# A C3-style block with attention and a pruned depthwise layer: the first pointwise convolution by seven quarter products, one reciprocal for two heads, and another order of pieces

## The chip, the cores and the metric

The kernel runs on one NeuronCore of one Trainium2 chip. The metric is the device time of one execution in microseconds. The kernel before was timed three times: 2596.55, 2593.97 and 2596.15 us, with a median of 2596.15 us. All data is fp32. The profile counts two MATMUL records, and two weight loads, for each fp32 matrix product that the program issues.

## The reference

For each of eight images x (512 channels, 32 by 32 pixels):

```python
x = x + conv_block(group_norm(x))
x = x + pruned_depthwise_block(group_norm(x))
```

The first block is what the change touches:

```python
t = silu(bn(conv1x1(x, cv1_w)))            # 512 -> 512 channels
ys = [t[:, :256], t[:, 256:]]
for i in range(2):
    z = silu(bn(conv3x3(ys[-1], m_cv1_w[i])))          # 256 -> 256
    q, k, v = conv1x1(z, m_qkv_w[i])                   # 4 heads of 64
    a = softmax(q.T @ (k + r) * 64 ** -0.5)            # 1024 x 1024 for each head
    z = silu(bn(conv1x1(a @ v, m_cv2_w[i])))
    ys.append(ys[-1] + z)
return silu(bn(conv1x1(concat(ys), cv2_w)))            # 1024 -> 512
```

The second block is a depthwise 3x3 convolution, a relu, a pruning by each channel's maximum, a 1x1 convolution from 512 to 512 channels, a relu and a second pruning.

## The kernel before

**Layout.** Channels lie on the 128 partitions in chunks, and the 1024 pixels of an image along the free dimension. The images are done one after another. The 3x3 convolutions use a transformed form (`conv3`, pieces `d`, `P`, `R`, `B`, `E`). The last 1x1 convolution of the first block for images 1 to 6 (`quartered`), and the 1x1 convolution of the second block for images 0 to 6 (`layer1_back` through `by_quarters` and `one_pair`), are done as seven products of quarters in place of eight, with sums of the quarters before and after. The weights' sums are made once in the first image, stored in DRAM (`combine_weights`, `combine_more`) and read back as tiles of a ring.

**The first 1x1 convolution, `cv1` (line 684).** All eight images do it as plain matrix products: for each of four output chunks m and each half n of the pixels, four products over the input chunks k. Chunks 2 and 3 (tiles `ps_cv1`) go to `yp[0]`, the input of the first 3x3 convolution; chunks 0 and 1 (tiles `ps_y0`) go to `y0`, which is not read until the last 1x1 convolution. The profile leaves out the numbers at the end of names, so `ps_cv1` and `ps_cv2` both stand as `ps_cv`, and `ps_y0` as `ps_y`.

**Attention (line 971).** One layer has 32 steps (two pairs of heads m, two halves of the queries ih, eight blocks of keys jt). Each step makes scores (`s`, four 64x64 matrix tiles side by side), exponentials on ScalarE (`e`), a running sum on VectorE (`p`) and the products with the values (`w`). For each pair of heads `n` then sums over the partitions with a matrix of ones (tile `ps_dn`), `nr` takes reciprocals in four pieces of 128 columns, `ns` spreads them over the partitions with two transfers through SyncE's queue (tile `rw`), `sc` scales z, and `nc` lets ScalarE check the range. The 1x1 convolution `m` of `cv2m` follows.

**Order.** Nothing schedules the work at run time. Every helper only appends pieces (small functions) to lists by a short name, and `go` (line 310) calls them in the order of a text: `FIRST` for image 0, `HEAD` and `TAIL` for images 1 to 6, `HEAD` and `LAST` for image 7. `HEAD` begins with the first 1x1 convolution of the image; the second block of the image before is spread through it (taps `t`, products `o` and `O`). `TAIL` holds the last 1x1 convolution (`Q`) and the normalisation of the next image (`g`, `ga`). The class `Engines` keeps TensorE, VectorE, ScalarE and SyncE in this order, so each is one queue; the waits between them follow from the tiles.

**Buffers.** PSUM has two double banks (`big`), three single banks (`acc`: the quarter products, the values, `m`) and one (`mm`: `ps_dn` and the small sums of the normalisations). SBUF has 11 work tiles and a ring of 5 weight tiles; `ring_load` issues the next transfer of `ring_sources` (line 388) when a tile has been used up.

Of the kernel before, what the change touches and what calls it, by code (L numbers as in the profile page):

```python
# [11 lines left out]
AF = mybir.ActivationFunctionType  # L12
# [3 lines left out]
P = 128  # L16
# [29 lines left out]
    g*6 gm gd gv g gp g gb gm gd ga gv ga c gp fo gb c ta0 ga ta0 ga ta0 ti0 fo ta2 to0*2 c  # L46
    ti0*2 ca ta2*2 c rl ca ta1*3 ti2 ti1 to1 d ti1 d y ya to1 ti1 y ya ti2 to2 d y ti2 d to2 rl
    ya y d*2 ya d P Rc R P d*3 Rc R d*2 P Rc R B P Rc R B*2 P*2 Rc R E Ez B Rc R E Ez k*2 X k dw
    ta0 ka k kp ka ta0*2 v kp ti0 v va ti0 v ti0 q v va ta1 q ta1 qa q*2 qa ta1 s e s e p to0 s
    e p w to0 s e w*2 ti1 s e p ti1*2 p s e p w s to1 s e p w e p w s w to1 ta2 e s e w h p z  # L50
    ta2 s e p ta2 s ti2 e w*2 s e w ti2 to2 ti2 s e w s e to2 w s e w s e w s e rh p w p*5 h z
    s*2 w e*2 n s e w p s p w nr e p w nr*2 s e nc s nr e ns p w s e p w*2 nc s e p w h z s e s
    w s*2 p*2 e w p e*2 p sc p w sc s w e p w s e p w*3 h z n nr*4 ns nc sc Q K m ma sc dp mr
    m*2 ma mr m ma mr ma mr d*4 Q nc K d*3 P d P Rc R d*2 Rc R d*2 P Rc R P*2 Rc B R B P Rc R E
    Ez Rc B*2 R E Ez k X dx k*3 ka*2 kp*2 v*2 q v*2 va*2 cw*3 rk cw q*2 qa q qa s*2 e*2 p s e p
    w s e w s p cw*2 e s e w s e p rk p w s e p*2 s e w s e g*2 w*2 p w h z s e w cw s e p*2
    cw*2 rk s e w*2 s e w s*2 p e rk w p s e g w p g p s*2 e g w g e*2 p w h z p s w e g p w n
    nr s e nr p w g s e s p w nr e s e w p w*2 s nr p e s e w h ns p s e p nc*2 s w e p w s e p
    w s e p w s sc e p s e p w sc w*3 h z n nr*2 Q nr*2 ns z Q sc*2 nc m*2 ma mr ma mr m ma nc m
    ma mr gm mr gd Q gv u A Q x u i A x i gp i*2 Q gb ga*4 Q im id Q iv A Q x ip i*2 ib b bm t*3  # L60
    Q A t x i*2
# [3 lines left out]
    t c*2 t b im id bm c ca iv t ip t l t*2 ib lr b t*3 c bm ca b y d y bm d ya d*2 ya d*3 y P d  # L65
# [60 lines left out]
def fast_kernel(  # L126
# [111 lines left out]

    r_dram = [dram.tile([P, 2, HW], F32, tag=f"r{l}", name="r") for l in range(2)]

    ones = const_tile([P, 32], "ones")
    nc.gpsimd.memset(ones, 1.0)

    rng = const_tile([P, B * 2 * HEADS], "rng")
# [1630 lines left out]
```

## Time and profile before

| | |
|---|---|
| median of three runs | 2596.15 us |
| the profiled execution, from its first to its last instruction (its span) | 2593.6 us |
| TensorE busy | 2557.7 us |
| VectorE busy | 2054.9 us |
| ScalarE busy | 1214.4 us |
| mean granted TensorE clock | 0.997 |
| DMA | 268.51 MB, 104 GB/s on average |

What the runtime adds around the profiled execution's span is not in the profile; the median of the runs is 2.55 us longer than this span. A duration in a row of the profile runs from an instruction's start to its end. TensorE and VectorE start the next instruction before the last has ended, so the distance between starts, and not the duration, is what an instruction costs in a full queue.

### The profile page before, as it was taken

To read this page: it belongs to the slowest core of one execution; us is meant where nothing else is said; L and a number is where in the kernel's file an instruction comes from. 1 tells how busy PE (TensorE), PEld (TensorE's weight loads), DVE (VectorE), ACT (ScalarE), POOL (GpSimd) and SP (SyncE) were. 2 spreads that over 40 slices of the span, in tenths; PEclk is the share of its full clock that TensorE was granted. 3 is DMA by queue.
4 is the path that set the end of the run, shared out by engine and by line. 5 is a ranking of instruction groups with operands and counts; after the bars stand their busy time and mean duration, and the time that the engine had idled before them with its cause. 6 is when DMAs were issued, how large, how long until landed. Compare 5 with 4: busy or idle time off the path is not lost.

```text
span 2593.6 us, 36377 instructions
## 1 busy us (share of the span) xinstructions
PE 2557.7 (99%) x14806; PEld 1292.0 (50%) x14806; DVE 2054.9 (79%) x2954; ACT 1214.4 (47%) x1551; POOL 129.2 (5%) x99
## 2 busy tenths in 40 slices
PE   8999999999999999999999999999999999999997
PEld 5454463634636346463464635545355544645443
DVE  8887588877897877877778778787788877888657
ACT  3635446353463544635445444544445454363534
POOL 1000000000100000000000000000001000010000
PEclk9999999999999999999999999999999999999998
DMA  9445230522305214060140702306122151312300
GB/s 347 157 155 203 66 122 25 167 98 73 113 27 199 66 65 122 17 247 18 65 122 17 248 18 81 105 24 241 33 96 75 61 204 34 130 45 82 122 17 34
DMA packets 83791, 268.51 MB, mean 104 GB/s; under 512 B 7072, under 2 KB 37536, under 8 KB 69408
## 3 DMA queue, kind: packets, MB, share of 16 engines
q1 hardware_dynamic: 76032, 248.01, 27.2%
q0 software_dynamic: 4032, 14.68, 3.1%
q10 hardware_dynamic: 3552, 3.41, 0.4%
q8 instruction: 118, 1.93, 0.3%
q14 instruction: 57, 0.47, 0.1%
HBM read 212.34 MB, written 36.96 MB: 96 GB/s over the span
## 4 chain that ended last, share of the span: by engine, by line
PE 95%; DVE 3%; ACT 1%; issue 0%; DMA 0%; SPq 0%; DVEq 0%; ACTq 0%
PE ps_av L105 16%; PE ps_s L105 16%; PE ps_c L105 13%; PE ps_cv L105 12%; PE ps_qk L105 8%; PE ps_cv2q L105 8%; PE ps_q L105 7%; PE ps_v L105 4%; PE ps_y L105 4%; PE ps_m L105 4%; PE ps_dn L105 1%; ACT qy L105 1%; DVE sum L105 1%; DVE ht L105 1%; PE ps_pw L105 0%
## 5 line engine op out<-in xcount | busy, mean ns | idle before, releaser
L105 ACT ACTIVATE e<-ps_s 128x1024 f32<-128x1024 f32 x512 | 509.7, 1023 | 286.8 <-PE ps_s L105 265.6
L105 PE MATMUL ps_s<-qy,kr 64*64 64x512 f32 x4096 | 513.7, 592 | 1.4
L105 DVE TENSOR_TENSOR sum<-sum,e 128x1024 f32<-128x1024 f32 x384 | 475.2, 1238 | 39.2 <-ACT e L105 19.9
L105 PE MATMUL ps_av<-e,vt 64*64 64x512 f32 x4096 | 506.2, 590 | 0.0
L105 DVE SCALAR_TENSOR_TENSOR ht<-xn,v_sb,ht 128x961 f32<-128x961 f32 (+1 forms) x256 | 317.3, 1247 | 8.6 <-ACT ht L105 5.0
L105 PEld LDWEIGHTS ps_s<-qy,kr 64*64 64x64 f32 x4096 | 160.5, 132 | 289.0 <-issue 191.1
L105 PEld LDWEIGHTS ps_av<-e,vt 64*64 64x64 f32 x4096 | 165.4, 133 | 277.4 <-issue 266.0
L105 PE MATMUL ps_qk<-z,wring 128*128 128x512 f32 x512 | 231.1, 596 | 2.0 <-ACT z L105 1.3
L105 DVE TENSOR_TENSOR sum<-e 128x1024 f32<-128x1024 f32 x64 | 78.1, 1220 | 164.0 <-ACT e L105 162.6
L105 ACT COPY c<-ps_c 128x256 f32<-128x256 f32 x96 | 35.6, 371 | 259.4 <-PE ps_c L105 259.3
L105 PEld LDWEIGHTS ps_qk<-z,wring 128*128 128x128 f32 x512 | 95.6, 190 | 115.7 <-issue 101.5
L105 DVE RECIPROCAL r<-ps_dn 128x128 f32<-128x128 f32 x128 | 113.7, 925 | 11.2 <-PE ps_dn L105 9.0
L105 PE MATMUL ps_c<-vt,wring 128*128 128x128 f32 x1024 | 119.4, 276 | 2.3 <-DVE v L105 1.3
L105 PEld LDWEIGHTS ps_c<-kr,wring 128*128 128x128 f32 x1024 | 116.8, 192 | 8.0 <-issue 6.1
L105 PEld LDWEIGHTS ps_c<-vt,wring 128*128 128x128 f32 x1024 | 116.2, 192 | 4.3 <-ACT c L105 2.3
L105 PE MATMUL ps_c<-qy,wring 128*128 128x128 f32 x1024 | 117.0, 275 | 0.0
L105 PE MATMUL ps_c<-kr,wring 128*128 128x128 f32 x1024 | 117.0, 275 | 0.0
L105 PE MATMUL ps_cv<-pt,w_sb 128*128 128x512 f32 x256 | 116.7, 607 | 0.0
L105 PE MATMUL ps_v<-wring,z 128*128 128x256 f32 x512 | 115.9, 379 | 0.7 <-DVE kr L105 0.7
L105 PEld LDWEIGHTS ps_c<-qy,wring 128*128 128x128 f32 x1024 | 115.6, 192 | 0.0
L105 PE MATMUL ps_m<-z,wm_sb 128*128 128x512 f32 x256 | 112.5, 592 | 0.0
L105 PE MATMUL ps_y<-pt,w_sb 128*128 128x512 f32 x256 | 112.3, 592 | 0.0
(178 smaller groups left out, 3255.5 us busy)
## 6 DMA issues: line engine op xcount, KB each, us to landing
wring<-u SPq DMA_DIRECT2D x96, 1024.0 KB, 4.8
pt<-in_x SPq DMA_DIRECT2D x32, 512.0 KB, 9.4
rw<-r SPq DMA_DIRECT2D x64, 256.0 KB, 3.4
xt<-in_x SPq DMA_DIRECT2D x32, 512.0 KB, 7.5
out<-xt SPq DMA_DIRECT2D x32, 512.0 KB, 8.0
kr<-r POOLq DMA_DIRECT2D x28, 512.0 KB, 6.6
wring<-q SPq DMA_DIRECT2D x14, 896.0 KB, 4.6
wring<-in_wqkv SPq DMA_DIRECT2D x16, 768.0 KB, 4.4
```

The source lines that it names most:

```text
L105: made = method(*args, **kwargs)
```

## The change

Five things are changed.

1. For images 1 to 7 the first 1x1 convolution is done as two times seven quarter products through `by_quarters` and `one_pair` (the new `quartered_cv1`; pieces `ct` for the sums of the input's quarters, `c ck cu ca` for the first pair of output chunks, `y yk yu ya` for the second). Image 0 keeps `cv1`. The sums of the weights are made in image 0 by a second `combine_more` and come through the ring: two more tiles of 896 KB for each later image. The sums of the inputs are written to the tile that held the plain weights (`w1_sb`), and to `z`.
2. The sums of the softmax (`sums`) put the four quarters of each head's 512 columns into four neighbouring partitions, with 16 products of 128 columns in place of 4 of 512; so one reciprocal of 128 columns (`reciprocal`) takes the place of four. `spread` needs eight transfers of 64 KB in place of two of 256 KB, and `check` reads 128 columns in place of 512.
3. A new piece `S` has ScalarE evaluate a Silu of one number ahead of the `ma` pieces, as `X` already does with Exp.
4. `ones` becomes 36 columns, of which every fourth is one.
5. The four texts of pieces stand in another order. `HEAD` and `TAIL` are shown here, `FIRST` and `LAST` change likewise.

```diff
...
 HEAD = """
-    t c*2 t b im id bm c ca iv t ip t l t*2 ib lr b t*3 c bm ca b y d y bm d ya d*2 ya d*3 y P d
-    Rc R d*2 P Rc R d ya P d Rc R B P Rc R P B*2 Rc R E P Ez Rc B R E Ez y k*3 ya k ka X lp ka
-    kd*2 t*5 v*2 l t va v*2 va t lr q*2 t*2 lp t q qa s q e qa s e p s t e w t s e w l s*2 p*2 w
-    e*2 p w s p e s w t s w t e s e p lr e p w*2 h z s e p w s t w s p s e p e*2 w*2 p s e w s t
-    e p s w p s e w e t p*2 w lp t h z s*2 e*2 w s*2 n e p*2 e w*2 s nr s p e w nr e p s e w nr
-    s nr t p ns l w e p*2 w lr lp w ot h s e s w p ot w s w s e*2 p*2 e w p s e w s e ot p*2 z
-    sc w nc w*2 h n nc o O nr ok Ok z nr*2 sc nr ns o ou oa O*2 Ou sc Oa m sc nc m*2 ma*2 m ma
-    mr ot mr ma mr o nc mr ou d Ou o O d ou Ou o d O ou*2 oa Ou*2 d Oa o O P d*2 Rc d*3 R P d*2
-    Rc R d P Rc P R B Rc P B Rc P R B*2 Rc R ou E oa Ou R Oa o O dp E Ez*2 X k v k v ou oa Ou
-    fr*2 Oa ka kd f*2 fr*2 f*2 dx va k v*2 k va q*4 ka kd qa*2 s*3 e*2 p e w p s e w s*2 e*2 p*3
-    w s*2 g e*2 w*2 s p e w*2 s e w p s*2 h g e g p w s w z p e*2 s w e g*2 s*2 w*2 p e*2 g p*3
-    g s w*2 e p s e w h s*2 e*2 p z p w*2 s p e p s n nr*3 w e s g e p w p s w*3 e p s nc e nr s
-    ns e nc w s h s p w z w e p s e w s p e*2 p sc s w e p*2 w s sc e p w*3 h n nr*4 ns z
+    c*4 ck cu ct*2 ca cu t im c cu*2 c*2 id iv cu y ca t cu*2 ca yk ca y*2 ip y t*2 d yu d ya y
+    ib yu d*2 P d yu d*2 b P Rc R b bm d P d*2 y Rc R Rc b d R d B P Rc l B lr R B P Rc R E B P
+    Rc R E Ez*2 yu bm*2 y lp yu ya yu*2 k t*19 v*2 va k*2 ya*2 ka k ka v*2 va X l kd q*2 qa lr lp
+    t kd q s e t q qa s e p w s e s e p w*2 s*2 e*2 w s*2 w*2 s e*2 w s w e*2 s p*5 h e l w s*2 w
+    e*2 lr t s w*2 p*2 e s e s e t w s w*2 z e s*2 e w e s w s*2 h e p e w s*2 p*5 z w e*3 s*2 e
+    t w e p*2 s*2 e*2 w*2 l lr w p ot s p*2 e p*3 lp w h z n nr nc ns p*2 w lp w s*2 w e s w*2
+    e*2 w*3 p sc p sc nc S p ot h z n nr o ok o ns O Ok ou oa ot*2 O sc m sc ma m ma Ou Oa m mr
+    ma m ma O o mr*3 Ou ou d o d ou o O*2 d*2 P Ou ou Ou d*2 o ou d Rc ou nc R oa d*2 Ou oa P Rc
+    d nc O P R d*2 P Rc P R B Oa Rc P R Ou Oa B*2 Rc B Rc R E R E Ez*2 o O k*4 ou oa Ou Oa ka*2
+    fr*3 v*2 va q*2 v*2 dp qa g va g q X kd f g f kd s e q qa fr f*2 dx s e w s*2 e w e s*2 w s*2
+    e*4 p*2 w s g*3 p*3 g s w*2 e s w*2 e*2 s*2 w g h s w e*2 w p*4 s*2 w s*2 w p*2 s*2 e p w e*6
+    p w*2 h s*2 e*2 z p*4 w p*2 s e s z e w p*2 s n nr ns e w*4 nc s nc s e w p e w h s*2 w sc w
+    e w s*2 e*3 w s p e p sc p*4 w*4 z n h z nr S ns
 """
 
 TAIL = """
-    Q*2 K r2 nc r0 Q r2 sc Q m r0 sc K m*2 ma nc mr ma m r0*2 ma mr r1*2 mr Q*3 ma mr r2 r1*2 u0
-    r2 a0 u1 gm a1 gd Q x1 u0 r3 gv x0 gp r3*2 u0 Q r3 gb u0*2 Q u0 a0 i a0 ga Q i x0*2 ga Q i
-    u0 a0 i im id ga Q iv ip u1 x0 Q u1*2 ib u1 b a1 x1 bm Q ga u1 t a1 i t Q x1 u1 i*2 a1 t i t
-    x1
+    r2 r0 Q*3 r0 sc*2 r0*2 m*2 r1 m ma gm m nc gd ma gv r1 ma r3 mr*2 K mr r2 r3 gp r2 ma mr r1
+    gb ga r1 K ga ct r2 Q r3 Q*4 u1 u0 r3 Q u0*4 Q u0 Q a1 Q a0 x0 a0 ga x0 i a0 x0 i*3 im u0 a0
+    id x1 ga ct Q iv ip Q u1 x0 ib b i u1 i bm t u1 t Q*2 u1 t*2 u1*2 a1 x1 a1*2 x1*2 i*2 nc
 """
 
...
@@ -238,8 +236,9 @@
 
     r_dram = [dram.tile([P, 2, HW], F32, tag=f"r{l}", name="r") for l in range(2)]
 
-    ones = const_tile([P, 32], "ones")
-    nc.gpsimd.memset(ones, 1.0)
+    ones = const_tile([P, 36], "ones")
+    nc.gpsimd.memset(ones, 0.0)
+    nc.gpsimd.memset(ones.rearrange("p (a b) -> p a b", b=4)[:, :, 3], 1.0)
 
     rng = const_tile([P, B * 2 * HEADS], "rng")
     rng_used = [0]
@@ -388,9 +387,9 @@
     def ring_sources():
         for b in range(B):
             for l in range(2):
-                if b and l:
+                if b:
                     for p in range(2):
-                        yield q_dram[1][p].rearrange("p q k o -> p (q k o)"), 1792
+                        yield q_dram[l][p].rearrange("p q k o -> p (q k o)"), 1792
                 for i in range(6):
                     yield u_dram[l][i].rearrange("p a b c d -> p (a b c d)"), 2048
                 yield wqkv[:, l].rearrange("p k o -> p (k o)"), 1536
@@ -721,6 +720,19 @@
         add("ca", *[lambda m=m: first_end(m) for m in (2, 3)])
         add("y", *[lambda m=m, n=n: half(m, n) for m in range(2) for n in range(2)])
         add("ya", *[lambda m=m, n=n: half_end(m, n) for m in range(2) for n in range(2)])
+
+    def quartered_cv1():
+
+        sums = [t.rearrange("p a b -> p (a b)") for t in (w1_sb, z)]
+        sums = [t[:, i * HW : (i + 1) * HW] for t in sums for i in range(2)]
+
+        def end(ps, p, low, n):
+            m = 2 * p + low
+            dst = inner(yp[0], low) if p else phases(y0[:, m, :])
+            act(dst[:, :, n * 16 : n * 16 + 16], by_phase(ps), AF.Silu, BN0 + m)
+
+        ends = [lambda ps, low, n, p=p: end(ps, p, low, n) for p in (1, 0)]
+        by_quarters((p_all, sums), ("ct", "c ck cu ca", "y yk yu ya"), ends)
 
     def conv3(l):
 
@@ -877,6 +889,7 @@
         add("Ez", *[lambda m=m: close(m) for m in range(2)])
 
         add("X", lambda: nc.scalar.activation(warm[:, 1:], warm[:, :1], AF.Exp))
+        add("S", lambda: nc.scalar.activation(warm[:, 1:], warm[:, :1], AF.Silu))
 
     def positions(l, m):
 
@@ -1030,31 +1043,37 @@
         def sums(m):
 
             dn = dns[m] = ps_mm.tile([P, 512], F32, tag="mm", name="ps_dn")
-            for i in range(4):
-                t = sm[m, i // 2]
-                nc.tensor.matmul(
-                    dn[32 * i : 32 * (i + 1), :], ones, t[:, i % 2, :], start=True, stop=True
-                )
-
-        def reciprocal(m, q):
-            if q == 0:
-                rr[m] = work_tile("r")
-            c = slice(q * 128, (q + 1) * 128)
-            nc.vector.reciprocal(rr[m][:, c], dns[m][:, c])
+            for j in range(4):
+                for i in range(4):
+                    nc.tensor.matmul(
+                        dn[32 * i : 32 * (i + 1), :P],
+                        ones[:, 3 - j : 35 - j],
+                        sm[m, i // 2][:, i % 2, j * P : (j + 1) * P],
+                        start=(j == 0),
+                        stop=(j == 3),
+                    )
+
+        def reciprocal(m):
+            rr[m] = work_tile("r")
+            nc.vector.reciprocal(rr[m][:, :P], dns[m][:, :P])
 
         def spread(m):
 
             wide = rs[m] = work_tile("rw")
             for ih in range(2):
-                twice = rr[m][half(ih), :512].unsqueeze(1).to_broadcast([HD, 2, 512])
-                nc.sync.dma_start(wide[:, ih * 512 : (ih + 1) * 512], twice)
+                for j in range(4):
+                    some = rr[m][ih * HD + j : (ih + 1) * HD : 4, :P]
+                    at = (4 * ih + j) * P
+                    nc.sync.dma_start(
+                        wide[:, at : at + P], some.unsqueeze(1).to_broadcast([HD // 4, 8, P])
+                    )
 
         def check(m, src):
 
             n = rng_used[0]
             rng_used[0] += 1
-            src = dns[m] if src == 0 else rr[m][:, :512]
-            nc.scalar.activation(rr[m][:, 512:], src, AF.Copy, accum_out=rng[:, n : n + 1])
+            src = dns[m][:, :P] if src == 0 else rr[m][:, :P]
+            nc.scalar.activation(rr[m][:, P : 2 * P], src, AF.Copy, accum_out=rng[:, n : n + 1])
 
         def scale(m, ih):
             c = slice(ih * 512, (ih + 1) * 512)
@@ -1069,7 +1088,7 @@
         add("h", *[lambda m=m, ih=ih: part(m, ih) for m, ih in both])
         add("z", *[lambda m=m, ih=ih: join(m, ih) for m, ih in both])
         add("n", *[lambda m=m: sums(m) for m in range(2)])
-        add("nr", *[lambda m=m, q=q: reciprocal(m, q) for m in range(2) for q in range(4)])
+        add("nr", *[lambda m=m: reciprocal(m) for m in range(2)])
         add("ns", *[lambda m=m: spread(m) for m in range(2)])
         add("nc", *[lambda m=m, i=i: check(m, i) for m in range(2) for i in range(2)])
         add("sc", *[lambda m=m, ih=ih: scale(m, ih) for m, ih in both])
@@ -1364,7 +1383,7 @@
 
         def decide():
             pk = ps_mm.tile([P, 512], F32, tag="mm", name="pk")
-            nc.tensor.matmul(pk[:1, :1], oks, ones[:, :1], start=True, stop=True)
+            nc.tensor.matmul(pk[:1, :1], oks, ones[:, 3:4], start=True, stop=True)
             nc.vector.tensor_scalar(flag, pk[:1, :1], P - 0.5, None, ALU.is_lt)
 
         add("rg", least, decide)
@@ -1390,12 +1409,11 @@
 
             add("rh", *[released] * 1)
             add("rk", *[lambda l=l, m=m: positions(l, m) for l in range(2) for m in range(2)])
+            combine_more(0, w1)
             combine_more(1, wpw)
             for p in range(2):
                 combine_weights(p)
             cv1(((2, (0, 1)), (3, (0, 1)), (2, (2, 3)), (3, (2, 3))))
-        else:
-            cv1(((2, (0, 1)), (2, (2, 3)), (3, (0, 1)), (3, (2, 3))))
         for l in range(2):
             conv3(l)
             qkv(l, first)
@@ -1403,6 +1421,7 @@
             cv2m(l)
         add("dx", lambda b=b: load(xt, b))
         if not last:
+            quartered_cv1()
             add("dp", lambda b=b: load(pt, b + 1))
             group_norm("g gm gd gv gp gb ga", pt, lambda c: pt[c], range(KC))
         if first:
```

## The prediction

> **What bounds the kernel.** I read the page first: busy time, then the chain that ended last.
>
> ```profile
> span 2593.6 us, 36377 instructions
> ...
> PE 2557.7 (99%) x14806; PEld 1292.0 (50%) x14806; DVE 2054.9 (79%) x2954; ACT 1214.4 (47%) x1551; POOL 129.2 (5%) x99
> ...
> PE 95%; DVE 3%; ACT 1%; issue 0%; DMA 0%; SPq 0%; DVEq 0%; ACTq 0%
> ```
>
> TensorE is busy for 99% of the span and carries 95% of the chain. VectorE's 79% is an average, so the next view is one period, from the end of one image's attention to that of the next, and the conv stage inside it (columns: stretch, its length, busy time of each engine):
>
> ```profile
> 653.30:688.70 35.40, 35.40 (x226) 27.71 (x225) 33.99 (x69) 12.87 (x24) 0.22 (x1) 1.00 0.45 157
> 583.28:899.49 316.21, 316.00 (x1846) 160.15 (x1845) 253.64 (x366) 149.50 (x192) 15.16 (x11) 1.00 0.29 96
> ```
>
> A period is 316.21 us with 0.21 us of TensorE idle. Overall VectorE has 62 us to spare, but in the first conv stage it is busy for 33.99 of 35.40 us. The chain in order of time shows the boundary (start, length):
>
> ```profile
> 639.31 6.87 PE ps_cv L105 x16
> 646.29 3.54 PE ps_cv L105 x8
> 649.95 3.54 PE ps_cv L105 x8
> 653.49 10.30 PE ps_y L105 x24
> 663.79 21.44 PE ps_c L105 x192
> 685.23 3.44 PE ps_y L105 x8
> ```
>
> Here cv1 has 16+8+8+24+8 = 64 records; eight take 3.44 us, 0.43 us each. The 13.7 us of `ps_y` are what TensorE does while VectorE prepares and finishes the 3x3 convolution. Then the sums of the softmax, and what follows the last one (VectorE, SyncE's queue and TensorE on their timelines):
>
> ```profile
> 558.64 1.90 PE L105 MATMUL ps_s<-qy,kr 64*64 64x512 f32 x16
> 560.46 1.07 PE L105 MATMUL ps_dn<-sum,ones 128*32 128x512 f32 x8
> 561.46 1.09 PE L105 MATMUL ps_av<-e,vt 64*64 64x512 f32 x8
> ```
> ```profile
> 899.56 3.39 DVE L105 RECIPROCAL r<-ps_dn 128x128 f32<-128x128 f32 x4 [1.29 <-PE ps_dn L105]
> ...
> 906.18 0.69 DVE L105 TENSOR_TENSOR z<-z,rw 128x512 f32<-128x512 f32 x1 [0.88 <-DMA rw<-r]
> ```
> ```profile
> 903.06 1.17 SPq L105 DMA_DIRECT2D rw<-r  x2
> ```
> ```profile
> 909.83 2.74 PE L105 MATMUL ps_m<-z,wm_sb 128*128 128x512 f32 x6
> ```
>
> Eight `ps_dn` records of 0.605 us each fill only 1.00 us from start to next start (560.46 to 561.46): four column strips run side by side. From the sums' end to the first `m` there are 10.4 us of other products, and the scaled z is there 3 us before it is wanted.
>
> **What the skill says.** "TensorE: Matmul & The Clock Gate", Part 3, says that products in different column groups of the array run at once, each starting some 4 ns after the last; the rows above agree (the trace has the four starts 7 ns apart). Its section "Back-to-back issue gap" says that weight loads matter more as products get shorter; here the 128-wide `ps_c`, each with its own load of 128 columns, cost 21.44/192 = 0.112 us against 0.107 for a quarter of 0.43, so a short product loses 4%. "DMA: Bandwidth & Descriptors", "Anatomy of one DMA", says that the fixed part of a transfer is mostly the wait for its completion; `rw` lands 3.4 us after issue at 256 KB and a ring tile 4.8 us at 1024 KB, which agrees: eight small transfers land hardly sooner than two larger ones.
>
> **The parts.**
>
> *Products.* 4 output chunks x 2 halves x 4 k = 32 become 2 x 7 x 2 = 28. Four fewer, eight records of 0.43 us: -3.44 us an image. Seven images: -24.0 us, on the path.
>
> *Sums on VectorE.* Added per image: four `ct` (the like `pt<-ht` row: 1.216 us) and fourteen adds (`kept<-kept,ps_q`: 0.679), 14.4 us by durations. Removed: three of four reciprocals, 16 times an image becoming 4, 12 x 0.925 = 11.1 us. The net +3.3 us is nothing beside 62 us of slack; where they stand is what matters. Queued VectorE work starts closer than its duration: four `kr<-v` take 2.43 us, 0.60 each for rows of 0.65 to 0.68.
>
> *The boundary.* I walk the new `HEAD` from the last `Q`, with 0.60 us for 512 columns, 1.15 for 1024, 0.33 for 256 on VectorE, 0.7 and 1.2 on ScalarE, and 0.4 for `Rc`. VectorE finishes `u1`, `x1`, `i` at 4.0 us, `ct` at 6.9, while TensorE does four products to 6.9. The three `acc` banks then set the pace: product five needs the bank of `a12`, free after `cu` and `ca` at 5.5, six that of `s2` (7.6), seven that of `s1` (9.3); TensorE comes at 6.9, 8.6, 10.3. No wait. The last `ca` stands behind `yk` in ScalarE's queue and ends at 15.2; two taps and `d d yu d yu d d` put the first input of `P` at 20.1, where TensorE has y's products until 20.6. Then P and y keep it until 45.5 (the loads of `d`, `yu`, `R`, `B` stay 0 to 3 us ahead of each P's buffer), the first `k` until 47.2, and the second `Ez` ends at 47.6: 0.4 us late for `v`. I take +0.4 x 7 = +2.8 us. If VectorE's steps cost their full durations, 12% more over some 44 us, the lag is 4 to 5 us, and the gain of an image is gone; that is the dear end.
>
> *Softmax sums.* 32 records of 128 columns for 8 of 512, 32 times. In four strips each strip has eight records of 0.112: 0.9 us plus the two changes of layout (about 0.2), as now. I take +0.05 us each, +1.6. If the strips did not overlap, 32 x 0.112 = 3.6 us, +2.5 each, +80 in all.
>
> *Spreading.* Reciprocal 3.39 to 0.95 us; SyncE then issues eight transfers at 0.59 us (1.17/2) instead of two. First half of z: after 0.95 + 0.1 + 4 x 0.59 it is issued, 3.2 later landed, 0.7 later scaled: 7.4 us after the sums; second half 9.7. Before `m` stand now `Q*3`, 8.6 us, where it was four pieces (10.4 us), so it holds by 1 us; the third `m` wants the second half at 12. In the first layer `o*2 O*2` give 6.9 us: 0.3 late, 7 times, +2.1. On SyncE only ring loads are queued behind, which wait for a used tile anyhow and land several products ahead. The ring: 21 tiles an image for 19; 1.8 MB more per image in 313 us is 6 GB/s on 96. Hidden; without that cover, a load is 4.8 us.
>
> *Tables.* The loads (1.28 us each, 34) mostly stand already in ScalarE's idle time; `S` is worth 0 to -2 us in all; I take -1.
>
> *Image 0.* `combine_more` again: 1 MB in, 14 stores, eight sums of 0.41 us, beside attention. It has several TensorE waits of about 1 us and the last image one of 4.7 (`ps_pw` waiting for VectorE, whose chain of taps after the last `x` keeps its length); another order can move these by +-4. I take 0.
>
> Sum on the span: 2593.6 - 24.0 + 2.8 + 1.6 + 2.1 - 1 = 2575.1; with the 2.55 us by which the median is above this span, 2577.6, say 2577.
>
> **Rivals.**
>
> *The wait hides better* (0.12): the walk's 0.4 and 0.3 vanish and the order closes some of image 0's waits: 2577 - 5 - 4 = 2568. For: the period before has 0.2 us of idle. Against: VectorE has more in a stage where it is already at 96%.
>
> *VectorE becomes the bound at the boundary* (0.13): 2 us of wait an image above the walk, +14: 2591; for 1 us, 2584. For: 33.99 of 35.40. Against: the second conv stage (`o`, `O`) already holds fourteen quarter products with their adds, without a wait.
>
> *The strips do not overlap for short products* (0.05): +80, 2655, slower. It decides from 24/32 = 0.6 to 0.75 us more per sum, that is when a group of four takes about twice its 0.112 us. Against: `ps_s` runs four tiles at once for long stretches.
>
> *The eight transfers come late* (0.04): each landing 2 us later than `rw` now, in both layers: 14 to 28 us, 2591 to 2605. Against: half the size issued before, and SyncE is idle there.
>
> My case (0.66) is 2577, itself 2570 to 2584. The range of 8 in 10 leaves out the strips, the late transfers and the ends: 2566 to 2591. This kernel's runs can tell about 0.2%, 5 us: faster is below 2590.9. Faster 0.88, same 0.04, slower 0.08.
>
> **What would show it.** The period falls to about 313.5 us, and the first convolution of all images from 512 records to 456. `ps_dn` of 128 columns: 1.0 to 1.1 us per 32 records if right, above 2 if the strips fail. At each boundary a TensorE idle of 0 to 0.5 us ahead of `ps_v`, put down to `z`; more, or idle ahead of `ps_c` put down to VectorE, is the second rival. Idle of `ps_m` on z or `rw` above 0.5 us is the fourth. Wrong altogether: a period at or above 316 us.

## The result, and the profile after

The changed kernel takes 2581.42 us (median of four runs, 2578.06 to 2582.45) beside 2595.47 us for the kernel before, timed beside it (four runs, 2593.97 to 2596.55). The ratio is 0.9945, with a 95% interval of 0.9931 to 0.9959: 14 us faster, and inside the predicted range. Its profiled execution has a span of 2580.4 us for 2593.6. The forecast was 2577, so the result is some 4 us to the slow side, and the two traces show that this is not one small miss but several large ones of both signs.

The page of the changed kernel, the same parts as shown of before:

```profile
span 2580.4 us, 38500 instructions
...
PE 2533.9 (98%) x15518; PEld 1329.0 (52%) x15518; DVE 2073.5 (80%) x2992; ACT 1207.6 (47%) x1595; POOL 126.2 (5%) x100
...
PE 72%; DVE 19%; DMA 3%; ACT 2%; issue 2%; SPq 1%; ACTq 0%; POOL 0%; DVEq 0%
```

TensorE lost 23.8 us of busy time (2557.7 to 2533.9), but the span lost only 13.2. The chain, 95% TensorE before, now runs through VectorE for 19% and through DMA for 3%. The stretches (length, then busy time of PE, PEld, DVE, ACT and POOL, the clock, the DMA share and GB/s) say where TensorE is still full:

```profile
591.74:904.98 313.24, 312.19 (x1936) 164.60 (x1940) 256.65 (x372) 148.87 (x198) 14.90 (x11) 1.00 0.31 103
640.00:714.00 74.00, 73.94 (x333) 47.29 (x331) 72.60 (x120) 34.12 (x49) 4.46 (x4) 1.00 0.42 135
```

One period, end of attention to end of attention, is 313.24 us here (316.21 before), with 1.05 us of TensorE idle (0.21 before). At the image boundary and in the first convolution after it VectorE is busy for 72.60 of 74.00 us. In the kernel before it was busy for 59.96 of 73.00 us there:

```profile
640.00:713.00 73.00, 72.92 (x355) 46.52 (x357) 59.96 (x100) 32.71 (x44) 7.30 (x5) 1.00 0.37 113
```

Most of the chain's 19% comes from this stage of each image; the end of it, in order of time (start, length):

```profile
693.68 1.34 DVE mid L103 x4
695.04 0.70 DVE y L103
695.77 1.25 ACT z L103
697.07 3.07 PE ps_v L103 x13
```

The chain follows VectorE's sums up to the last `y`, then ScalarE's `z`, then `ps_v`. Yet TensorE waits for almost nothing there: between the starts of its products, one gap of 0.22 us ahead of the `ps_v` at 697.07. VectorE and TensorE are ready at almost the same time: the second rival of the prediction, VectorE as the bound at the boundary, is close, but TensorE does not wait for it yet.

To see where the 13.2 us come from I cut each execution at the end of the last product with the values (`ps_av`) of each attention. All columns in us:

| kernel | image 0, to the end of its first attention | from there to the end of its second | image 1 | mean of images 2 to 7 | tail | span |
|---|---|---|---|---|---|---|
| before | 146.03 | 124.60 | 311.66 | 316.24 | 113.83 | 2593.6 |
| after | 148.96 | 133.45 | 309.33 | 312.90 | 111.30 | 2580.4 |
| difference | +2.93 | +8.85 | -2.33 | -3.34 | -2.53 | -13.2 |

Six periods give 6 x 3.34 = 20.0 us. Image 0 takes back 11.8. So most of what is to be explained lies in the first 283 us, where the prediction had put a zero.

The chain of the changed kernel in the second attention of image 0:

```profile
224.44 7.51 DMA ht<-in_w
...
233.57 5.58 DMA xt<-in_x
239.18 10.08 DMA ht<-in_w
...
250.91 4.31 DMA r<-pos
...
255.33 1.03 ACT e L103
```

The chain runs through transfers, one behind the other, with next to no computing between. ScalarE's timeline has the price at the end of each entry (idle before it, and what ended it):

```profile
245.93 1.94 ACT L103 ACTIVATE e<-ps_s 128x1024 f32<-128x1024 f32 x2 [4.99 <-DMA s<-scomb]
...
255.33 1.03 ACT L103 ACTIVATE e<-ps_s 128x1024 f32<-128x1024 f32 x1 [5.66 <-DMA r<-pos]
```

An exponential needs a work tile to write to. There are 11, and the sums of weights (`scomb`) and the positions (`pos`) hold theirs until their transfers have landed. ScalarE waits 4.99 and 5.66 us, and TensorE then stands idle for 2.12 and 4.88 us ahead of the scores that wait for these exponentials.

### The profile page after: what moved, and what is told of

Same layout as the page of the kernel before. It is cut to its first block, busy times and chain, and to the rows that moved or that the text cites. A ratio compares the mean times of both kernels' runs of the same rounds, so it can differ in the third digit from the quotient of the medians.

```text
span 2580.4 us, 38500 instructions
## 1 busy us (share of the span) xinstructions
PE 2533.9 (98%) x15518; PEld 1329.0 (52%) x15518; DVE 2073.5 (80%) x2992; ACT 1207.6 (47%) x1595; POOL 126.2 (5%) x100
## 4 chain that ended last, share of the span: by engine, by line
PE 72%; DVE 19%; DMA 3%; ACT 2%; issue 2%; SPq 1%; ACTq 0%; POOL 0%; DVEq 0%
PE ps_s L103 15%; PE ps_av L103 14%; PE ps_qk L103 8%; PE ps_c L103 7%; PE ps_q L103 7%; PE ps_cv L103 6%; PE ps_cv2q L103 6%; PE ps_m L103 4%; PE ps_v L103 4%; DVE ht L103 3%; DVE mid L103 2%; DVE sum L103 2%; SPq L103 1%; DVE y L103 1%; DVE vtmp L103 1%
## 5 line engine op out<-in xcount | busy, mean ns | idle before, releaser
L103 ACT ACTIVATE e<-ps_s 128x1024 f32<-128x1024 f32 x512 | 504.9, 1024 | 238.3 <-PE ps_s L103 194.7
L103 PE MATMUL ps_av<-e,vt 64*64 64x512 f32 x4096 | 518.3, 593 | 0.0
L103 DVE TENSOR_TENSOR sum<-sum,e 128x1024 f32<-128x1024 f32 x384 | 468.5, 1220 | 58.3 <-ACT e L103 31.0
L103 PEld LDWEIGHTS ps_av<-e,vt 64*64 64x64 f32 x4096 | 185.1, 133 | 254.3 <-issue 227.5
L103 PEld LDWEIGHTS ps_s<-qy,kr 64*64 64x64 f32 x4096 | 172.2, 132 | 278.6 <-issue 131.3
L103 PE MATMUL ps_q<-pt,wring 128*128 128x512 f32 x392 | 176.8, 594 | 0.0
L103 PEld LDWEIGHTS ps_q<-pt,wring 128*128 128x128 f32 x392 | 71.7, 190 | 81.0 <-issue 69.4
L103 ACT ACTIVATE m<-ps_m,bi,sc 128x512 f32<-128x512 f32 x64 | 50.0, 781 | 134.7 <-PE ps_m L103 133.6
```

The costliest lines, as they stand in the source:

```text
L103: made = method(*args, **kwargs)
```

## The experiments

The first theory on the loss in image 0 (theory 1): the loads and stores of the weight sums follow one another in SyncE's queue and through one half of one tile, and so hold work tiles. Its rival (theory 2): the eight added sums on VectorE hold it up. The other questions were what each part is worth alone, and a start-up that was longer in some kernels than in others. The stages of every experiment, read as above (in e4 only those of the fast part, as told there). Each row is one execution. The periods of a kernel agree within 2 us, but the first part of image 0 varies more from kernel to kernel, so differences of about 1 us in image 0 are not read as effects:

| kernel | image 0, first part | image 0, second part | image 1 | mean of 2 to 7 | tail | span |
|---|---|---|---|---|---|---|
| e1 | 151.51 | 124.41 | 311.31 | 316.46 | 112.73 | 2598.7 |
| e2 | 147.69 | 129.65 | 312.84 | 315.34 | 111.18 | 2593.4 |
| e3 | 147.59 | 127.48 | 309.23 | 312.88 | 111.60 | 2573.2 |
| e4 | 149.38 | 131.20 | 309.24 | 313.02 | | |
| e5 | 146.08 | 131.94 | 309.31 | 312.77 | 111.60 | 2575.5 |
| e6 | 150.13 | 124.65 | 311.70 | 316.26 | 112.67 | 2596.7 |
| e7 | 149.58 | 123.55 | 309.46 | 312.60 | 112.62 | 2570.8 |
| e8 | 147.88 | 132.57 | 309.66 | 313.40 | 111.12 | 2581.6 |
| e9 | 146.89 | 123.57 | 309.36 | 312.70 | 113.01 | 2569.1 |
| e10 | 145.94 | 123.37 | 309.34 | 312.80 | 112.58 | 2568.0 |
| e11 | 149.13 | 124.70 | 311.69 | 316.27 | 113.21 | 2596.4 |
| e12 | 151.09 | 127.47 | 312.46 | 315.58 | 112.28 | 2596.8 |

### e1: the second part alone

The kernel before with the new `sums`, `reciprocal`, `spread` and `check`, and the `ones` that they need; the order stays, and of the four pieces `nr` for a pair of heads three do nothing.

```diff
-    ones = const_tile([P, 32], "ones")
-    nc.gpsimd.memset(ones, 1.0)
+    ones = const_tile([P, 36], "ones")
+    nc.gpsimd.memset(ones, 0.0)
+    nc.gpsimd.memset(ones.rearrange("p (a b) -> p a b", b=4)[:, :, 3], 1.0)
...
-        add("nr", *[lambda m=m, q=q: reciprocal(m, q) for m in range(2) for q in range(4)])
+        add("nr", *[(lambda m=m: reciprocal(m)) if q == 0 else (lambda: None) for m in range(2) for q in range(4)])
```

> The kernel before with the second part of the change alone: 16 short products, one reciprocal, eight transfers; the order of pieces is that of before, and the one reciprocal stands where the first of the four stood. If this part costs the path nothing (the sums still take 1.0 us of TensorE, and VectorE's saved 11 us an image lie off the path): within 3 us of before. If the four strips do not overlap: 60 to 80 us slower. If VectorE was what the path waited for: 10 us or more faster.

Measured: 2599.24 us, ratio to before 1.0015 (1.0008 to 1.0022). A period is 316.46 us for 316.24 before: taking 11 us of VectorE's work from an image gains nothing in the old order, as TensorE was not waiting for it. But the kernel is slower, and the whole of it stands in the first part of image 0: 151.51 for 146.03. The loss stands ahead of the first attention, where no softmax has run yet: the first product with the values starts at 97.5 us for 92.3. This was the first sign of a second cause in image 0; e5, e6 and e11 follow it.

### e2: the second part undone

The changed kernel with the old block from `sums` to `check` and the old `ones`; the piece `nr` calls the four old reciprocals.

```diff
-        add("nr", *[lambda m=m: reciprocal(m) for m in range(2)])
+        add("nr", *[lambda m=m: [reciprocal(m, q) for q in range(4)] for m in range(2)])
```

> The changed kernel with the second part alone undone: four reciprocals and two transfers for each pair of heads, in the new order of pieces. If the new order relies on the sooner reciprocal: in the first layer of each image only 6.9 us of products stand between the sums and the first m, and with four reciprocals z is scaled about 1.5 us too late, so 8 x 1.5 = 12 us slower than the changed kernel, 2593 us, with TensorE idle ahead of ps_m or VectorE waiting for rw there. If VectorE's saving lies off the path in this order as well: 2581, no wait there.

Measured: 2598.61 us, ratio to before 1.0013 (1.0007 to 1.002), so 17 us slower than the changed kernel. With the old `ones` of 32 columns it also has the tiles where the kernel before had them, which e5 will show to be worth 3 us; beside e5 it is 20 us slower. A period is 315.34 us for 312.90. The same part that gains nothing in the old order (e1) is worth 2.44 us an image in the new one, because the new order gives the reciprocal no time. ScalarE and then TensorE behind the first sums of an attention in image 2:

```profile
765.50 0.60 ACT L103 ACTIVATE r<-ps_dn 128x512 f32<-128x512 f32 x1 [4.12 <-DVE r L103]
766.08 1.93 ACT L103 ACTIVATE e<-ps_s 128x1024 f32<-128x1024 f32 x2
```
```profile
767.15 1.09 PE L103 MATMUL ps_s<-qy,kr 64*64 64x512 f32 x8 [1.10 <-ACT e L103]
```

ScalarE takes its instructions in order. Its range check (`nc`) waits 4.12 us for VectorE's four reciprocals, the exponentials stand behind it, and TensorE waits 1.10 us for them. Each of images 2 to 7 has this wait and one of 0.68 us in its second attention, 1.78 us together, where the changed kernel has none of them but for one of 0.34 us. All of TensorE's idle time in a period is 1.87 us for 0.63 (mean of images 2 to 7), so some 1.2 of the 2.44 us are idle time and the rest is not placed. The parts of a change don't add up like prices of single articles.

### e3: the image's load later

The changed kernel with one word of `FIRST` moved: `dx`, the four loads of `xt`, stands behind the last weight sums. (The text is wrapped anew; these are the lines with the word.)

```diff
-    va q rk q qa q cw s e cw q qa s e p w s*2 e p e p w cw s*2 dx w e p s e p e s e p*2 w*3 s e w
...
+    s*2 e w s e w s g*2 s w p s*2 e*2 cw e cw w*2 e s p*2 w*2 s*2 cw w p*2 e p e*3 rk p cw*2 dx h
```

> The changed kernel, with one piece of FIRST moved: dx, the four loads of the first image for the second block, goes from between two weight combinations to behind the last of them. Theory 1 (SyncE's queue and the transfers hold up the second attention of image 0): the fourth load of weights lands in 7.5 us in place of 10 and is issued 2.5 us sooner, so image 0 gets 3 to 6 us shorter, 2576 us. Theory 2 (VectorE's extra sums hold it up): no change, 2581. Theory 3 (the order of e, p and w in FIRST is at fault by itself): no change.

Measured: 2578.01 us, ratio 0.9936 (0.9919 to 0.9952). The intervals of e3 and of the changed kernel overlap, so the time alone does not settle it; the trace does. The second part of image 0 goes from 133.45 to 127.48 us, 6.0 less, and the periods stay (312.88). No work was removed, only 2 MB of transfers taken out from between the loads of the weights. The two waits of 4.99 and 5.66 us become one of 3.17, again on `r<-pos`.

### e4: no sums of the first convolution's weights on VectorE

```diff
-                for r in range(2):
-                    nc.vector.tensor_tensor(part(name, r), part(x, r), part(y, r), op)
+                if i == 1:
+                    for r in range(2):
+                        nc.vector.tensor_tensor(part(name, r), part(x, r), part(y, r), op)
```

This kernel leaves out the eight sums of `combine_more(0, w1)` and their work tiles, and stores plain quarters where the sums belong, so images 1 to 7 use other weights. The values then leave the range that the kernel tests at its end, and its general version, compiled in behind the fast one, runs as well: 8235 us in all. Only the stages of the fast part are read.

> The changed kernel without the eight sums over the weights of the first convolution on VectorE, and without the two work tiles that held them; the plain quarters are stored in their place, so all 14 stores and the load stay. What it leaves out: the sums of these weights, so the first convolution of images 1 to 7 is another. Theory 1 (transfers): image 0 stays as long, at most 2 us shorter, 2579 to 2581. Theory 2 (VectorE's sums): 5 to 8 us shorter, 2574.

Measured: the second part of image 0 takes 131.20 us, 2.25 less than with the sums, while the loads stand where they stood (the second is issued at 210.0 us for 209.4). e5 and e8, which change nothing in this stage's pieces, take 131.94 and 132.57 us, so part of the 2.25 may be chance. VectorE's sums and the two tiles that they held are a quarter of the loss at the most; e3 gave back 6.0 with all of them there. Theory 2 falls as the main cause.

### e5, e6 and e11: where the tiles stand

`ones` grew from 32 to 36 columns. Tiles are laid out one behind the other, each padded to 32 bytes, so what is allocated later moved by 32 bytes: the ring of weight tiles from 171008 to 171040 and the work tiles from 125952 to 125984 in each partition, off the multiple of 256 bytes on which both stood. e5 takes the changed kernel and pads `ones`, so that both stand on a multiple of 256 again; e6 and e11 take the kernel before, whose instructions stay the same, and shift these tiles by 32 and by 64 bytes.

```diff
e5, on the changed kernel:
-    ones = const_tile([P, 36], "ones")
+    ones = const_tile([P, 96], "ones")[:, :36]
e6, on the kernel before:
-    ones = const_tile([P, 32], "ones")
+    ones = const_tile([P, 36], "ones")[:, :32]
e11, on the kernel before:
-    ones = const_tile([P, 32], "ones")
+    ones = const_tile([P, 48], "ones")[:, :32]
```

> The changed kernel with the tile of ones allocated with 96 columns, of which the first 36 are used as now: every tile allocated after it stands 256 bytes further on than in the kernel before, in place of 16 bytes, and nothing else differs. Question: why the kernels with the new block of sums start slower (transfers u<-ucomp 4.3 to 4.6 us in place of 3.2 to 3.3, the TensorE gap on wring<-u at 50 us 2.9 to 3.8 us in place of 1.5 to 1.7). If the ring and work tiles stand badly because of the 16 bytes, the landing of u<-ucomp returns to about 3.3 us, the gap to about 1.5 us, and the time falls by 2 to 4 us to 2577.5 to 2579.5, more if the transfers in the second attention of image 0 gain too. If the 16 bytes mean nothing (rival), the start-up and the time are those of the changed kernel, 2581.4 within 1 us.

> The kernel before with the tile of ones allocated with 36 columns, of which the first 32 are used as now: every tile allocated after it stands 16 bytes further on; no instruction differs. If the 16 bytes slow the transfers, it is 3 to 5 us slower than the kernel before (2598.5 to 2600.5), as e1 was, with u<-ucomp landing in 4.3 to 4.6 us and the gap at 50 us at 3 to 3.8 us; then all of the loss of e1 is this. If they mean nothing, it equals the kernel before within 0.5 us.

> The kernel before with the tile of ones allocated with 48 columns, of which the first 32 are used. In the kernel before the ring and work tiles stand at multiples of 256 bytes; in the changed kernel and e6 32 bytes past one (the allocation rounds 144 bytes up to 160, so the shift is 32 bytes and not the 16 that the expectations of e5 and e6 name); here 64 bytes past one. If a start off a multiple of 256 bytes is what costs, it is 3 to 4 us slower than the kernel before, as e6 was, with a gap on wring<-u at 50 us above 3 us. If a start at a multiple of 64 bytes is enough, it equals the kernel before within 0.7 us, with a gap of about 1.5 us.

Measured: e6 2598.4 us, ratio to before 1.0012 (1.0005 to 1.0018); e11 2599.07 us, 1.0013 (1.0006 to 1.002). Both are slower by 3.4 and 3.7 us, with not an instruction changed, and in both only the first part of image 0 is longer, by 4.1 and 3.1 us; every later stage agrees with before within 0.1 us, but for the tail. (The expectations of e5 and e6 name 16 bytes; with the padding it is 32.) So 64 bytes is no better than 32. e5 takes 2578.32 us, ratio 0.9935 (0.9922 to 0.9949): the interval overlaps that of the changed kernel, but the trace has the first part of image 0 at 146.08, that of before. e1, 4.3 us slower than the kernel before beside it, has the same shift and loses in the same place; e1 with the tiles put back was not run.

How it comes about, in the start-up, where the DMA engines are busy throughout (a share of 1.00 from 25 to 60 us). Transfers issued in this time in the kernel before (size, median us from issue to landing):

```profile
wring<-u SPq DMA_DIRECT2D x6, 1024.0 KB, 6.5
u<-ucomp SPq DMA_DIRECT2D x11, 256.0 KB, 3.2
```

and in e6:

```profile
wring<-u SPq DMA_DIRECT2D x6, 1024.0 KB, 9.0
u<-ucomp SPq DMA_DIRECT2D x11, 256.0 KB, 4.1
```

The transformed weights are stored from work tiles (`u<-ucomp` and `u<-uplane`) and read back into the ring (`wring<-u`). From 25 to 29 us these stores, in packets of 1024 bytes, are all that moves. The last number is GB/s, in the kernel before and then in e6:

```profile
25.00:29.00 4.00, 4.00 (x11) 1.75 (x10) 3.93 (x7) 2.32 (x3) 0.00 (x0) 1.00 1.09 383
```
```profile
25.00:29.00 4.00, 4.00 (x11) 1.85 (x10) 3.93 (x8) 2.44 (x3) 0.00 (x0) 1.00 1.01 341
```

So the stores themselves are 11% slower. All kernels with the tiles on a multiple of 256 (before, e2, e5, e9, e10) have 383 or 384 GB/s here; those with a shift (the changed kernel, e1, e3, e4, e6, e7, e8, e11, e12) have 340 or 341. The packets of 8192 bytes that fill the ring are not slower: 346 ns each on average from 25 to 60 us before, 334 in e6. Later landings end in a wait of the first 3x3 convolution of e6:

```profile
54.54 1.78 PE L105 MATMUL ps_c<-vt,wring 128*128 128x128 f32 x9 [4.26 <-DMA wring<-u]
```

and in the kernel before, at that place:

```profile
52.33 3.92 PE L105 MATMUL ps_c<-vt,wring 128*128 128x128 f32 x33 [1.29 <-DVE v L105]
```

The wait is 3.0 us longer, the stage 4.1. Stretch 43 to 70 us of the kernel before:

```profile
43.00:70.00 27.00, 25.07 (x201) 22.90 (x200) 25.26 (x57) 6.77 (x17) 0.00 (x0) 1.00 0.88 318
```

and of e6:

```profile
43.00:70.00 27.00, 22.74 (x189) 22.58 (x188) 21.14 (x47) 4.82 (x13) 0.00 (x0) 0.94 0.87 315
```

The granted clock is 1.00 with the short wait and 0.94 with the long one, which fits the rest. The Trainium skill, "DMA: Bandwidth & Descriptors", "How a descriptor splits into AXI transactions", says that a transaction starts at a multiple of 256 bytes, so that a row starting elsewhere takes one more and fetches bytes that it does not use. For a row of 1024 bytes, as `ucomp` is stored, I estimate from it five transactions in place of four, but in the section's beats of 32 bytes only 33 in place of 32. The 11% lie between the two, so the section agrees in direction and does not give the size; no run shows the transactions. The landing grew more than the rate fell, by 28% in e6 and, at 4.5 us, by 41% in e11; that part may be transfers queued behind others.

### e7: two buffers for the weight sums

In the changed kernel all four loads of weights to be combined go into the second half of `h_all`. In e7 they alternate between `x_all` and `h_all`; `cw` is split into the load (`cl`), the plain stores (`cs`) and the sums (`cw`), and in `FIRST` each load stands well ahead of its sums, and `dx` behind the last that reads `x_all`. Of the four, the two in `combine_more` are edited like this, the two in `combine_weights` alike:

```diff
-        w = h_all[:, 2:, :].rearrange("p a b -> p (a b)").rearrange("p (k o) -> p k o", o=C)
+        w = (h_all if i else x_all)[:, 2:, :].rearrange("p a b -> p (a b)")
+        w = w.rearrange("p (k o) -> p k o", o=C)
...
+        add("cl", load)
+        add("cs", plain)
         add(
             "cw",
-            load,
```

> The changed kernel where the four sums of weights in the second attention of image 0 no longer follow one another through the same half of one tile: they alternate between two tiles, each load is issued well before its sums, and the image's next load stands behind the last sums. By the first theory (the loads, one behind the other in SyncE's queue, hold the work tiles and with them the exponentials), the stage loses 6 to 9 us against the changed kernel and the time is 2572.5 to 2575.5, at or below e3 (2578.0). If e3 had only moved a wait by chance (rival), the time is that of the changed kernel, 2579 to 2584.

Measured: 2573.22 us, ratio 0.992 (0.9906 to 0.9933). The second part of image 0 takes 123.55 us: 9.9 less than in the changed kernel and 1.1 less than before, with four blocks of weight sums where before had three. The whole loss of that stage was the way its transfers were queued and its buffer shared, and none of it the work itself. Theory 1 holds. How much of it is the queue and how much the shared half-tile was not separated; e3, which changes the queue alone, gave back 6.0.

### e8: no tables loaded ahead

```diff
-        add("S", lambda: nc.scalar.activation(warm[:, 1:], warm[:, :1], AF.Silu))
+        add("S", lambda: None)
```

> The changed kernel without the piece S, that is, without the early evaluation of Silu that loads its table ahead of time; nothing else differs. The prediction took this part as worth 0 to 2 us, 1 us in the sum: 2581.4 to 2583.4. If ScalarE's table loads stand on the path at each of the fourteen places where S stood (rival), about 1.28 us each: up to 18 us slower, 2599.

Measured: 2586.41 us, ratio 0.9971 (0.996 to 0.9982), 5.0 us slower than the changed kernel. In the trace a period is 313.40 us for 312.90. From the end of the first 3x3 convolution to the end of the last attention the loss is 2.9 us. So 3 to 5 us, where the prediction took 1 of "0 to 2", and far from the 18 of the rival: the loads do not stand on the path whole. `S` is called sixteen times (the expectation says fourteen), so each is worth 0.2 to 0.3 us of a load's 1.28.

### e9 and e10: the two mended, and all tiles at multiples of 256 bytes

e9 is e7 with the `ones` of e5. e10 adds a pad ahead of the first tile and lengthens `v_sb`, so that `pt`, `xt`, `ht`, `w1_sb`, `z`, `kr`, `qy` and `vt` stand on such a multiple too, and pads `ones` to 88 columns so that ring and work tiles stay on one.

```diff
+    const_tile([P, 24], "pad")
     p_all = const_tile([P, KC, HW], "pt")
...
-    v_sb = const_tile([P, V_N], "v_sb")
+    v_sb = const_tile([P, V_N + 52], "v_sb")[:, :V_N]
...
-    ones = const_tile([P, 96], "ones")[:, :36]
+    ones = const_tile([P, 88], "ones")[:, :36]
```

> The changed kernel with the edits of e7 (weight sums of the second attention of image 0 from two buffers, the next image's load behind them) and of e5 (ring and work tiles again at multiples of 256 bytes). If the two causes are independent, their gains add: 8.2 us and 3.1 us from 2581.4 give 2570, with 2567.5 to 2572. If the aligned tiles gain part of the same time that the second buffer gains (in e5 1.2 us of its 4.4 in the trace came from that attention), 2571 to 2573.2.

> e9 with all large SBUF tiles at multiples of 256 bytes: a pad of 96 bytes ahead of the first, and v_sb lengthened by 208 bytes. In all kernels so far pt, xt and ht stand 160 bytes past such a multiple, the raw weights, w1_sb, z, kr, qy and vt 224. The instructions are the same. If the start-up is short of transfers because of their starts (89% of the DMA engines' time is busy in the first 70 us), the loads of x and of the raw weights gain as the ring's did, and it is 1 to 4 us faster than e9. If only the ring's own landing counts (rival), it equals e9 within 1 us.

Measured: e9 2569.1 us (2568.62 to 2571.01), ratio to before 0.9897 (0.9882 to 0.9912): 26 us faster than before, 12 faster than the changed kernel, and its interval lies clear of the latter's. The two gains alone, 8.2 us in e7 and 3.1 in e5, make 11.3, so the two causes add within the noise. e10 takes 2570.03 us (2568.26 to 2570.52), the same as e9: the tiles that count are the ring's and the work tiles', not those of the long rows. In its trace the first part of image 0 is 0.95 us shorter, but the time does not show it.

Stretches of the second attention of image 0 in the changed kernel:

```profile
195.00:240.00 45.00, 44.61 (x291) 19.64 (x292) 32.99 (x41) 23.10 (x25) 4.07 (x2) 1.00 0.73 241
240.00:262.00 22.00, 15.01 (x116) 4.72 (x112) 18.40 (x19) 7.46 (x9) 0.00 (x0) 0.85 0.77 264
```

and in e9:

```profile
195.00:240.00 45.00, 44.68 (x308) 19.81 (x312) 33.97 (x43) 22.58 (x24) 4.07 (x2) 1.00 0.88 289
240.00:262.00 22.00, 21.65 (x228) 7.52 (x220) 19.00 (x19) 13.59 (x17) 0.00 (x0) 1.00 0.41 144
```

In the changed kernel TensorE is idle for 7 of 22 us from 240, and the clock is down to 0.85 after waits of 2.12 and 4.88 us. In e9 the transfers are done earlier (a DMA share of 0.88 ahead of 240 us, 0.41 after it), and TensorE has 0.35 us idle at a full clock.

### e12: the first part undone

The changed kernel with plain `cv1` for all images, without `combine_more(0, w1)` and the ring's two tiles; the pieces of the quarter products are taken from the new texts and the eight plain ones put there by hand.

```diff
-            combine_more(0, w1)
...
+        else:
+            cv1(((2, (0, 1)), (2, (2, 3)), (3, (0, 1)), (3, (2, 3))))
...
-            quartered_cv1()
```

> The changed kernel with its first part undone: plain cv1 for all images, no third and fourth weight sums for it in image 0, two ring tiles fewer per later image, the pieces of it taken out of the new order and the plain ones put in their place. Everything else is as changed. By the theory, 7 times 3.3 us of products come back and the 8 to 10 us that the weight sums cost in the second attention of image 0 go away: 2581.4 + 23 - 9 = 2595, with 2592 to 2598 (hand-made order of the boundary: up to 3 us more). If the steady gain came from the new order and not from the products (rival), the time stays at 2572 to 2582.

Measured: 2595.26 us, ratio to before 0.9998 (0.999 to 1.0006): without its first part the change as it stands is worth nothing. That is a sum of two signs, for e12 keeps the shift of the tiles. In its trace, of the slowest of its runs, the two parts of image 0 take 5.1 and 2.9 us more than before, and the later images and the tail 4.7 us less. Beside the changed kernel image 0's second part gives back 6.0 us (127.47), and a period is 315.58 us for 312.90, 2.68 more. The stage from the end of an image's second attention to the end of the next first attention takes 183.98 us on the mean of images 2 to 7; the changed kernel has 181.04, the kernel before 184.01. So the gain of that stage is that of the quarter products alone, 2.94 us, and the rest of the period's gain, 0.4 us, lies behind it. e12 has that rest too (0.6 us), so it belongs to the other parts of the change; which of them was not found.

## Why the prediction was right, and where not

The ledger in spans: predicted -18.5 us, measured -13.2. Image 0 is +11.8 for 0. Images 1 to 7 are -2.33 - 20.04 = -22.4 for -24.0 + 2.8 + 1.6 + 2.1 = -17.5. The tail is -2.5, where the tables' -1 (spread over all images) was all that the sum had. The differences, +11.8 - 4.9 - 1.5, make the +5.3 between 2575.1 and 2580.4.

*Products* and *The boundary*: right. They were to give 3.44 - 0.4 = 3.04 us an image together; the stage gives 2.94 by e12. The records are as counted: `ps_q` from `pt`, `z` and `w_sb` has 392 + 112 + 112 = 616, less the 224 of the second block 392; with 64 of image 0 that is 456. Of the walk's 0.4 us the trace has 0.33 at the very instructions named, the `ps_v` behind the last `Ez`: from start to next start they take 14.14 us an image (mean of images 2 to 7), where the kernel before and e12 have 13.81. The queues that the walk looked at, three banks and VectorE at 0.60 us per 512 columns, foresaw this.

*Softmax sums*: right. The rows of the changed kernel (busy and mean ns of one):

```profile
L103 DVE TENSOR_TENSOR z<-z,rw 128x512 f32<-128x512 f32 x64 | 46.8, 732 | 62.4 <-DMA rw<-r 62.0
...
L103 PE MATMUL ps_dn<-sum,ones 128*32 128x128 f32 x1024 | 37.7, 276 | 4.4 <-DVE sum L103 4.4
...
L103 DVE RECIPROCAL r<-ps_dn 128x128 f32<-128x128 f32 x32 | 30.4, 949 | 7.0 <-PE ps_dn L103 7.0
```

1024 records of 276 ns fill 37.7 us, for 40.3 with 256 of 605 ns, so the strips run side by side. The busy time is not the price, though: from the first start of a sum to the next product 24 of the 32 sums take 1.01 us, where 23 of those before took 1.00; the others hold waits. That is +0.01 for the +0.05 of the step. The third rival is out.

*Spreading*: the place was wrong and the size too. I had assumed that eight small transfers land 3.2 us after issue, "hardly sooner" than two larger ones. The row of the transfers (size, median us from issue to landing):

```profile
rw<-r SPq DMA_DIRECT2D x256, 64.0 KB, 2.0
```

They land in 2.0 us; the larger ones took 3.4. So TensorE shows no wait at `ps_m` (its weight loads wait 2.5 us in all for z, and no product behind them). Instead VectorE, which takes its instructions in order, stands at `z<-z,rw` for the first of the eight and then for the fifth, and what is queued behind is late. Around the last sum of the first layer in image 2:

```profile
769.67 0.69 DVE L103 TENSOR_TENSOR z<-z,rw 128x512 f32<-128x512 f32 x1 [1.40 <-DMA rw<-r]
770.28 1.22 DVE L103 TENSOR_TENSOR sum<-sum,e 128x1024 f32<-128x1024 f32 x1
772.24 0.69 DVE L103 TENSOR_TENSOR z<-z,rw 128x512 f32<-128x512 f32 x1 [0.73 <-DMA rw<-r]
772.84 1.22 DVE L103 TENSOR_TENSOR sum<-sum,e 128x1024 f32<-128x1024 f32 x1
```

and TensorE there:

```profile
772.71 0.41 PE L103 MATMUL ps_dn<-sum,ones 128*32 128x128 f32 x4
774.12 1.07 PE L103 MATMUL ps_dn<-sum,ones 128*32 128x128 f32 x28 [0.99 <-DVE sum L103]
```

The second half of the sum over the partitions waits 0.99 us for a `sum` that stood behind `z<-z,rw`. This is most of the 1.05 us of idle in that period. Over the whole kernel TensorE's row has 4.4 us for it, where the step had 2.1 at `ps_m`. I had named what is queued behind the transfers on SyncE, but not what is queued behind the multiplication on VectorE. The period shortens by more than predicted all the same: TensorE's busy time in it fell by 3.81 us, the 3.44 of the products and 0.37 that I can't place.

*Tables*: undersized. 3 to 5 us for 1, by e8.

*Image 0*: the step that failed. It counted the added work ("1 MB in, 14 stores, eight sums of 0.41 us, beside attention") as hidden, with 4 us to either side, and the stage lost 8.85 us. The work was hidden indeed: e7 does all of it in less time than before. What was not hidden was its queue: four loads through one half-tile, each waiting for the stores of the one before, with the next image's 2 MB between them, and work tiles held meanwhile that the exponentials need. Nor was it all the added work's: e12, without that work, still takes 127.47 us in this stage for 124.60 before, 2.9 us that come with the new order. The prediction followed queue and tiles for the ring and for `spread`, where they cost little, and skipped them here. The other 2.93 us are the start-up, for which no step of the prediction asked: the fourth edit, four more columns of `ones`, cost about as much as the third, the tables, gave.

The tail's 2.5 us were not tested. By TensorE's timeline, the wait of 4.7 us on `ps_pw` near the end of before is gone, and one of 2.6 us at the normalisation is new: another order of `LAST`, within the +-4 of the step.

Of the 2.55 us by which the median stood above the profiled span before, the changed kernel shows 1.0, as its profiled execution is the slowest of the four; this took 1.5 us off the error by chance. That the forecast is off by 4 us only is luck in part: image 0's loss of 11.8 us, for which the sum had a zero, met images and a tail that were 6.4 us better than the sum.

## What to carry to other kernels

Cost a block of one-time work by its queue and its buffers, not only by its engine time: ask which transfer it is issued behind, which tile it fills again, and who needs the tiles that it holds. Where an engine takes its instructions in order, a wait is paid by what stands behind it. A part that gains nothing alone can be what makes a new order possible, so undo it in the new order before you drop it. And a change of a small tile's size can move all tiles behind it: look at the addresses.

## What the runs showed of the hardware

A shift of ring and work tiles by 32 or 64 bytes off a multiple of 256 cost 3.4 and 3.7 us in a kernel with not an instruction changed. The time is lost ahead of the first product with the values (96.2 and 95.2 us for 92.3), where stores in packets of 1024 bytes ran at 341 GB/s for 383. With the tiles at the next multiple of 256 (e5) the first part of image 0 takes 146.08 us, for 146.03 before. In all later stages of the kernel before, the tail left out, the same shift changed 0.1 us at most.

Eight transfers of 64 KB, issued 0.6 us apart, land in 2.0 us each, where two of 256 KB took 3.4. The section "Anatomy of one DMA" of the Trainium skill's "DMA: Bandwidth & Descriptors", which is written for transfers that GpSimd issues, led me to read the fixed part as nearly all of it; here, on SyncE's queue, the size still counted.

A TensorE wait of 3.3 to 4.9 us came with a lower granted clock in its stretch: 0.94 from 43 to 70 us for waits of 3.3, 3.7 and 4.3 us in the changed kernel, e7 and e6, and 0.85 from 240 to 262 us. Waits of 1.3 and 1.2 us in the kernel before and e5 did not (1.00). Between these it went both ways in the same stretch: 1.00 with 2.5 and 2.8 us in e8 and e3, 0.87 with 2.7 us in e12. So a long wait can cost more than its length.
